# Four-direction convolution scan on one core: the DRAM layout of the inputs and of layer 0's results, and what is transferred in one DMA

## The chip, the cores and the metric

One core of a Trainium2 chip runs the whole program in one launch. The metric is device time in microseconds (us). Three runs of the kernel before took 4221.05, 4223.90 and 4226.26 us, so the median is 4223.9 us.

## What is computed

The input `x` has 32 images of 48 channels, 64 rows and 128 columns, in float32. Two layers follow each other. Each adds to `x` a chain of four scans over its group-normalised input (16 groups of three channels, over the whole image):

```python
def step(w, b):
    def f(carry, inp):
        nxt = inp + _conv1d(carry, w, b)     # 5 taps, 48 channels to 48
        return (nxt, nxt)
    return f
...
_, d_rest = jax.lax.scan(step(down_w, down_b), d0, xs[1:])     # over rows, downwards
_, u_rest = jax.lax.scan(step(down_w, down_b), u0, seq)        # over rows, upwards
_, r_rest = jax.lax.scan(step(right_w, right_b), r0, ws[1:])   # over columns, to the right
_, l_rest = jax.lax.scan(step(left_w, left_b), l0, R[Ww - 2::-1])
...
x = x + _L0_conv_ref(_gn(x), ...)
x = x + _L1_conv_ref(_gn(x), ...)
```

A scan is serial: row h needs row h-1 of the same scan. A row scan convolves along the width, a column scan along the height.

## The kernel before

The images are taken in four groups of eight. A row phase does the scan down and up of one group (126 steps of nine 128x128 products on TensorE, each record a half of a float32 product, so 18 records a step, and three adds on VectorE at L865). A column phase does the scans to the right and left of a pair of groups (254 steps). `PHASES` gives the order of the twelve phases: rows 0-0, rows 0-1, columns 0-0, rows 0-2, rows 1-0, rows 0-3, columns 0-1, rows 1-1, rows 1-2, rows 1-3, columns 1-0, columns 1-1, where the first number is the layer and the second the group or pair. The text below counts them from 0. The tiles of TensorE's results bear the names: `step_02d` is layer 0, group 2, downwards, phase 3; `step_11d` is phase 7.

SBUF holds three slots of rows. In a row phase a partition is a pair of (column modulo 8, channel), and 8 x 48 = 384 pairs fill three tiles of 128, `o` = 0, 1, 2. In a column phase a partition is a pair of (row modulo 8, channel). The change from one to the other goes through DRAM, in runs of 32 numbers (128 bytes), which are 4 columns of 8 images. Because 48 channels do not divide 128, a tile consists of three or four `PIECES` (48, 32 or 16 partitions), ten in the three tiles, and most transfers are made piece by piece.

The DRAM tensors in question are `xin` (the permuted input of each group, layer 0's source), `mid` (layer 0's result, layer 1's source), and `upa` and `upb` (the results of the row phases of layers 0 and 1). They are touched by:

- `move_rows` (L657): loads or stores blocks of eight rows for a row phase, one DMA for each piece, so ten DMAs for eight rows and 80 for a group's 64 rows. Each has four quarters of the width in it. A store for the seam between a row and a column phase gives the quarter `q` and takes a quarter alone.
- `scale_rows` (L688): ScalarE normalises 16 loaded rows in place, 24 instructions.
- `load_residual` (L776) and `keep_result` (L790): in a column phase they bring a unit of the source and take a unit of the result to `mid`. A unit is one quarter, one group of the pair and one tile of 128 partitions, with 8192 bytes a partition. They issue one DMA for each piece, three or four in a unit. `load_residual` issues on the queue of SyncE (SP) in layer 0 and on that of ScalarE (ACT) in layer 1, all the others on SP.
- `x_put` and `put_out`: write the permuted input to `xin`.

The order of the work is written by hand. `at(t, ...)` places work at a step number, the agenda is sorted by it, and `in_order` chains the instructions of each engine in that order. A step number thus only sets the place in an engine's queue. SP runs ahead of TensorE where nothing holds it. `plan_rows` places the loads in four lots of 16 rows at `t0 + ahead[i]` and their scaling at `t0 + scaled[i]`. A DMA on SP or ACT waits for one of eight completion semaphores, which the two queues use in turn, so that it also waits for the landing of the DMA that had its semaphore last.

`first_group` (L1145 on) is written out by hand for the first group: it loads eight rows directly in a form with 48 partitions (`top`, in two sets), moves them to their places by products with shifted identities (`place_kernel`, L1210, and `rows_by_product`, L1243), and does the statistics, the permutation and the first rows in between.

Of the kernel before, what the change touches and what calls it, by code (L numbers as in the profile page):

```python
# [29 lines left out]
F32 = mybir.dt.float32  # L30
# [3 lines left out]
C = 48  # L34
# [8 lines left out]
E8 = 8  # L43
# [76 lines left out]
def kernel(  # L120
# [62 lines left out]
    mask_in = wt["left"].rearrange("p i n -> p (i n)")[:, 5 * FULL : 5 * FULL + NG * C]  # L183
# [4 lines left out]
    def kept(name):  # L188

        return [  # L190
            dram.tile([C, CHANNEL + PAD], F32, tag=f"{name}{g}", name=f"{name}{g}")[:, 0:CHANNEL]
            for g in range(NGRP)
        ]

    source = [
        [
            dram.tile([E8 * NQ, C, UNIT], F32, tag=f"xin{g}", name=f"xin{g}")
            for g in range(NGRP)
        ],
        kept("mid"),  # L200
    ]
    ups = [kept("upa"), kept("upb")]
    taps = [
# [23 lines left out]
    def x_by_row(t, e, h0, h1):  # L227

        t = t.rearrange("(i q) c (a e n) -> e a c i q n", i=E8, a=NH, e=E8)[e, h0 // E8]
        return t[:, h0 % E8 : h0 % E8 + h1 - h0].rearrange("c i q n -> c (i q) n")  # L230

    def x_by_col(t, e, j):


        return t[e * NQ + j]

    def x_put(t, r):


        t = t.rearrange("(i q) c (a n) -> i (c a) q n", i=E8, a=NH)[r % E8]  # L240
        return t.rearrange("(p r) q n -> r p q n", r=PR // E8)[r // E8]

    def by_col(t, e, j):
# [108 lines left out]
    def scaling(key, layer, g, averages, masks, slack=0):  # L352
# [41 lines left out]
        if not slack:  # L394
            far = ps[:, 1 + NG : 2 + NG]
            nc.vector.tensor_tensor(far, mean_p, ps[:, 0:1], ALU.subtract)
            nc.vector.tensor_tensor(dev, mean_p, ps[:, 0:1], ALU.subtract)
            nc.vector.tensor_tensor(far, far, dev, ALU.mult)
            nc.vector.tensor_tensor(dev, far, var_p, ALU.add)
            yield  # L400
            expand(var, dev[:, 0])
            yield
            nc.vector.tensor_scalar(var, var, GN_EPS, None, ALU.add)
            r0 = small("std")
            nc.scalar.activation(r0, var, AF.Sqrt)
            expand(mean, mean_p[:, 0])
            yield
            yield
            nc.vector.reciprocal(r0, r0)
            nc.vector.tensor_tensor(var, var, r0, ALU.mult)  # L410
            nc.vector.tensor_tensor(var, var, r0, ALU.mult)
            nc.vector.tensor_scalar(var, var, -0.5, 1.5, ALU.mult, ALU.add)
            nc.vector.tensor_tensor(scale, var, r0, ALU.mult)
            nc.vector.tensor_tensor(offset, mean, scale, ALU.mult)
            nc.vector.tensor_scalar(offset, offset, -1.0, None, ALU.mult)
            return
# [237 lines left out]
    def row(k, h):  # L654
        return row_views(k)[h // HALF][:, :, h % HALF]

    def move_rows(k, h0, h1, to_dram, q=None):  # L657

        _, layer, g = PHASES[k]
        view = row_views(k)[h0 // HALF]  # L660
        t = (ups if to_dram else source)[layer][g]
        for h in range(h0, h1, E8):
            end = min(h1, h + E8)
            for o in range(NG):
                for e, c0, c1, p0 in pieces(o):
                    here = view[p0 : p0 + c1 - c0, o, h % HALF : h % HALF + end - h]
                    if to_dram or layer:
                        there = by_row(t, e, h, end, q)[c0:c1]
                    else:
                        there = x_by_row(t, e, h, end)[c0:c1]  # L670
                    if q is None:
                        here = here.rearrange("p h (q n) -> p (h q) n", q=NQ)
                    else:
                        here = here[:, :, q * RUN : (q + 1) * RUN]
                    if to_dram:
                        dma(there, here)
                    else:
                        dma(here, there)
# [97 lines left out]
    def load_residual(k, j, i, nat):  # L776
        _, layer, pair = PHASES[k]
        o, half = UNITS[i]
        t = source[layer][2 * pair + half]
        for e, c0, c1, p0 in pieces(o):  # L780
            here = nat[p0 : p0 + c1 - c0]
            there = (by_col if layer else x_by_col)(t, e, j)[c0:c1]
            dma(here, there, nc.scalar if layer else None)

    def add_residual(k, j, i, nat, eng=nc.gpsimd):
        o, half = UNITS[i]
# [3 lines left out]
    def keep_result(k, j, i):  # L790
        _, layer, pair = PHASES[k]
        o, half = UNITS[i]
        for e, c0, c1, p0 in pieces(o):
            dma(
                by_col(source[1][2 * pair + half], e, j)[c0:c1],
                quarter(k, j)[p0 : p0 + c1 - c0, half, o],
            )

    def by_image(t):

# [344 lines left out]
    def first_group():  # L1145
# [3 lines left out]

        shift = wt["left"].rearrange("p i n -> p (i n)")  # L1150
        start = 7 * C // 3
        whole = shift[:, 0 : 2 * FULL + start - C // 3 + ODD]
        part = shift[:, whole.shape[-1] : whole.shape[-1] + FULL + ODD]
        SETS = ((0, C), (ODD, ODD + C))

        def selects(piece, s=0):
            e, c0, c1, o, p0 = piece
            t, at = (part, 0) if c0 and p0 else (whole, start - p0 + c0)
            p, q = SETS[s]
            return t[p:q, at + p : at + p + FULL]  # L1160

        rows = PR // 2
        four = E8 // 2
# [2 lines left out]
        stats = InputStats("x0", GB)  # L1166
        n = W * GB

        kernel = slot[slots(0)[0]][0:C, 0 : TAPS * C + 6]
        zeros = slot[slots(0)[0]][0:C, 512 : 512 + NG * FULL + 6]  # L1170

        def load_kernel():
            nc.vector.memset(zeros, 0.0)
            for j in range(TAPS):
                d, si = divmod(TAPS - 1 - j, 2)
                to = kernel[:, j * C : (j + 1) * C]
                dma(to, w[SIDES[si], 0, DOWN, d, SIDES[0]], nc.scalar if j % 2 else nc.sync)
            aside(kernel[:, TAPS * C :], bias[0:C].rearrange("c l k -> c (l k)"))

        def make_ident():  # L1180
            nc.vector.memset(shift[:, 0 : whole.shape[-1] + FULL + ODD], 0.0)
            for t, base in ((whole, start), (part, 2 * C - C // 3)):
                nc.gpsimd.affine_select(
                    t,
                    t,
                    pattern=[[1, t.shape[-1]]],
                    compare_op=ALU.not_equal,
                    fill=1.0,
                    base=-base,
                    channel_multiplier=-1,  # L1190
                )
            nc.gpsimd.memset(part[:, 0 : 2 * C], 0.0)
            nc.gpsimd.memset(part[:, 2 * C - C // 3 + ODD : 2 * C + ODD], 0.0)

        def place_kernel():
            for i in range(NG):
# [181 lines left out]
```

## Time and profile before

| what | us |
|---|---|
| median of three runs | 4223.9 |
| the profiled execution's own time | 4228.38 |
| its span | 4226.6 |
| TensorE busy | 4086.4 (97%) |
| first scan step on TensorE | 62.3 |
| last record of a step on TensorE | 4143.8 |
| phase 1 starts (tile `step_01d`) | 334.7 |
| phase 3 starts (`step_02d`) | 1096.5 |
| phase 4 starts (`step_10d`) | 1367.0 |
| phase 5 starts (`step_03d`) | 1619.3 |
| phase 7 starts (`step_11d`) | 2381.1 |
| phase 8 starts (`step_12d`) | 2643.7 |
| phase 9 starts (`step_13d`) | 2892.7 |
| phase 10 starts (`step_10r`) | 3141.8 |

The starts are the first records of these tiles on TensorE. Phase 8 and phase 9 have no wait in them and took 249.0 and 249.1 us for 126 steps, hence 1.976 us a step. The timeline of SP shows each group of DMA instructions with its start, the time from its first to its last end, its tensors and a count. The time of such a group divided by its count is the time that the queue gives to one DMA.

### The profile page before, as it was taken

The numbers are of one execution on the slowest core, as the hardware profiler recorded it, in microseconds if no ns is written. First come the engines' busy times: TensorE is split into PE (matmuls) and PEld (weight loads), VectorE is DVE, ScalarE is ACT, GpSimd is POOL, SyncE is SP. The second block draws the span as 40 slices with busy tenths as digits, with TensorE's granted clock in tenths as the row PEclk, the third lists the DMA queues.
The fourth block names the chain that finished last, engine by engine and source line by source line (L and its number), as shares of the span: only waits on it lengthen the run. The fifth ranks groups of instructions, "written<-read, shape, count | busy, mean of one in ns | idle before, by whom it ended". The sixth has DMA issues, their size and how long they took to land. (4 is left out here: it accounts for less than half of the span.)

```text
span 4226.6 us, 90155 instructions
## 1 busy us (share of the span) xinstructions
PE 4086.4 (97%) x36724; PEld 4055.0 (96%) x36724; DVE 2135.8 (51%) x6501; ACT 1287.5 (30%) x2525; POOL 791.2 (19%) x737
## 2 busy tenths in 40 slices
PE   8999999999999999999999999999999999999992
PEld 6999999999999999989999999999999999999992
DVE  5454444456644454444457654444444444444443
ACT  6844000536874633000016854503000012110122
POOL 3520010334322100010023310000000034410352
PEclk9999999999999999999999999999999999999996
DMA  9987669659979997259419979759188059899999
GB/s 293 236 174 115 110 126 209 216 148 250 208 187 172 199 151 126 41 102 202 84 48 265 203 144 156 114 80 161 32 147 182 1 99 246 236 260 156 177 202 182
DMA packets 2118431, 680.55 MB, mean 161 GB/s; under 512 B 2006416, under 2 KB 2056832, under 8 KB 2079616
## 3 DMA queue, kind: packets, MB, share of 16 engines
q1 hardware_dynamic: 2015504, 582.07, 69.0%
q10 hardware_dynamic: 99952, 87.20, 9.7%
q0 software_dynamic: 2560, 5.51, 0.5%
q8 instruction: 289, 4.73, 0.5%
q14 instruction: 126, 1.03, 0.1%
HBM read 397.77 MB, written 295.14 MB: 164 GB/s over the span
## 5 line engine op out<-in xcount | busy, mean ns | idle before, releaser
L688 ACT ACTIVATE arena<-arena,offset,scale 128x256 f32<-128x256 f32 (+2 forms) x840 | 582.3, 788 | 310.4 <-DMA arena<-mid 176.8
L788 POOL TENSOR_TENSOR arena<-arena 128x2048 f32<-128x2048 f32 x80 | 362.9, 4548 | 1442.6 <-PE step_10l L856 461.4
L637 POOL COPY arena<-arena 128x256 f32<-128x256 f32 x332 | 196.7, 660 | 443.1 <-DMA arena<-in_x 394.2
L575 ACT ACTIVATE early<-arena 128x256 f32<-128x256 f32 x192 | 129.5, 674 | 453.6 <-DMA arena<-xin 315.2
L856 PE MATMUL step_01r<-arena,early 128*128 128x128 f32 x2286 | 254.2, 275 | 10.0 <-DMA arena<-arena 5.4
L856 PEld LDWEIGHTS step_01r<-arena,early 128*128 128x128 f32 x2286 | 253.3, 187 | 10.9 <-DVE arena L865 6.0
L856 PE MATMUL step_00r<-arena,early 128*128 128x128 f32 x2286 | 253.5, 275 | 8.7 <-DMA arena<-arena 4.4
L856 PEld LDWEIGHTS step_00r<-arena,early 128*128 128x128 f32 x2286 | 252.8, 186 | 9.4 <-issue 4.8
L856 PE MATMUL step_11r<-arena,early 128*128 128x128 f32 x2286 | 251.5, 274 | 5.5 <-DVE arena L865 5.5
L856 PEld LDWEIGHTS step_11r<-arena,early 128*128 128x128 f32 x2286 | 251.0, 185 | 5.9 <-DVE arena L865 5.8
L856 PE MATMUL step_00l<-arena,wleft 128*128 128x128 f32 x2286 | 249.3, 272 | 0.0
L856 PE MATMUL step_01l<-arena,wleft 128*128 128x128 f32 x2286 | 248.7, 272 | 0.1
L856 PEld LDWEIGHTS step_00l<-arena,wleft 128*128 128x128 f32 x2286 | 248.7, 184 | 0.0
L856 PEld LDWEIGHTS step_01l<-arena,wleft 128*128 128x128 f32 x2286 | 248.4, 184 | 0.3 <-DVE arena L865 0.3
L856 PE MATMUL step_10l<-arena,wleft 128*128 128x128 f32 x2286 | 248.5, 272 | 0.0
L856 PE MATMUL step_10r<-arena,early 128*128 128x128 f32 x2286 | 248.5, 272 | 0.0
L856 PE MATMUL step_11l<-arena,wleft 128*128 128x128 f32 x2286 | 248.5, 272 | 0.0
L856 PEld LDWEIGHTS step_10l<-arena,wleft 128*128 128x128 f32 x2286 | 248.4, 184 | 0.0
L856 PEld LDWEIGHTS step_10r<-arena,early 128*128 128x128 f32 x2286 | 248.4, 184 | 0.0
L856 PEld LDWEIGHTS step_11l<-arena,wleft 128*128 128x128 f32 x2286 | 248.4, 184 | 0.0
L813 ACT COPY arena<-arena 128x256 f32<-128x256 f32 x172 | 99.5, 655 | 409.0 <-POOL arena L788 154.1
L260 ACT COPY early<-arena 128x1 f32<-128x1 f32 x2 | 0.4, 192 | 655.0 <-DVE arena L865 655.0
(200 smaller groups left out, 7090.7 us busy)
## 6 DMA issues: line engine op xcount, KB each, us to landing
xin<-arena SPq DMA_DIRECT2D x91, 512.0 KB, 4.2
arena<-in_x SPq DMA_DIRECT2D x18, 2048.0 KB, 11.0
arena<-xin SPq DMA_DIRECT2D x96, 384.0 KB, 8.7
mid<-arena SPq DMA_DIRECT2D x96, 384.0 KB, 8.1
arena<-mid SPq DMA_DIRECT2D x192, 192.0 KB, 4.3
upb<-arena SPq DMA_DIRECT2D x192, 192.0 KB, 3.9
arena<-upb SPq DMA_DIRECT2D x96, 384.0 KB, 12.4
arena<-xin SPq DMA_DIRECT2D x180, 192.0 KB, 4.3
```

The costliest lines, as they stand in the source:

```text
L260: fn(*args)
L575: nc.scalar.activation(junk[:, 0:n], view[:, b], AF.Identity, accum_out=self.sum[:, i, j : j + 1])
L637: copy(dst[:, r, q], src[:, r0 + r, q])
L688: nc.scalar.activation(args[0], args[0], AF.Identity, bias=args[2], scale=args[1])
L788: eng.tensor_tensor(unit, unit, nat, ALU.add)
L813: copy(by_w(perm)[:, a], src[:, a])
L856: nc.tensor.matmul(part(whole(ps[o])[0:m], -s), weights[:, i, at : at + m], part(src(i), s), start=seen[o] == 1, stop=seen[o] == left[o],)
```

## The change

- `xin` of groups 1 to 3 and `mid` of all groups are laid out as (quarter, (row modulo 8, channel), position), `whole`, instead of ((row modulo 8, quarter), channel, position) and (channel, all the rest). Group 0 keeps its layout (`first_x`). A unit is then one block with one partition after the other: `by_unit` gives it in one DMA, or in two for `o` = 2.
- `load_residual` and `keep_result` use `by_unit`; for group 0's `xin` the old pieces stay.
- `move_rows` loads a piece with four DMAs, one for each quarter, except for group 0. Stores are as before.
- `plan_rows` no longer issues 16 rows in one lot: it places six lots of one `o` and eight rows, 1.3 steps apart, from two steps earlier.
- The products of `first_group` contract over 128 partitions instead of 48, with zeros in the rest; for this the weights' place, the identities and two ranges of 32 partitions of `top` are cleared first.
- In `scaling` without slack, the products for the mean are issued before the square root and not after it.

```diff
+    def whole(name, g):
+        return dram.tile([NQ, E8 * C, UNIT], F32, tag=f"{name}{g}", name=f"{name}{g}")
+
+    first_x = dram.tile([E8 * NQ, C, UNIT], F32, tag="xin0", name="xin0")
     source = [
-        [
-            dram.tile([E8 * NQ, C, UNIT], F32, tag=f"xin{g}", name=f"xin{g}")
-            for g in range(NGRP)
-        ],
-        kept("mid"),
+        [first_x] + [whole("xin", g) for g in range(1, NGRP)],
+        [whole("mid", g) for g in range(NGRP)],
     ]
...
-    def x_by_col(t, e, j):
-        return t[e * NQ + j]
+    def by_quarter(t, e, h0, h1, q):
+        t = t[q].rearrange("(i c) (a e n) -> e a c i n", i=E8, a=NH, e=E8)[e, h0 // E8]
+        return t[:, h0 % E8 : h0 % E8 + h1 - h0]
+
+    def by_unit(t, o, j):
+        at = [(o * FULL, 0, FULL)]
+        if o == NG - 1:
+            at = [(6 * C, 0, 2 * C), (5 * C + C // 3, 2 * C, FULL)]
+        return [(t[j, r : r + p1 - p0], p0, p1) for r, p0, p1 in at]
...
             expand(var, dev[:, 0])
+            expand(mean, mean_p[:, 0])
             yield
             nc.vector.tensor_scalar(var, var, GN_EPS, None, ALU.add)
             r0 = small("std")
             nc.scalar.activation(r0, var, AF.Sqrt)
-            expand(mean, mean_p[:, 0])
...
-    def move_rows(k, h0, h1, to_dram, q=None):
+    def move_rows(k, h0, h1, to_dram, q=None, groups=range(NG)):
...
-            for o in range(NG):
+            for o in groups:
...
-                    if to_dram or layer:
+                    if to_dram:
                         there = by_row(t, e, h, end, q)[c0:c1]
+                    elif t is first_x:
+                        there = x_by_row(t, e, h, end)[c0:c1]
                     else:
-                        there = x_by_row(t, e, h, end)[c0:c1]
+                        for n in range(NQ):
+                            dma(
+                                here[:, :, n * RUN : (n + 1) * RUN],
+                                by_quarter(t, e, h, end, n)[c0:c1],
+                            )
+                        continue
...
-        for e, c0, c1, p0 in pieces(o):
-            here = nat[p0 : p0 + c1 - c0]
-            there = (by_col if layer else x_by_col)(t, e, j)[c0:c1]
-            dma(here, there, nc.scalar if layer else None)
+        queue = nc.scalar if layer else None
+        if t is first_x:
+            for e, c0, c1, p0 in pieces(o):
+                dma(nat[p0 : p0 + c1 - c0], t[e * NQ + j][c0:c1], queue)
+        else:
+            for there, p0, p1 in by_unit(t, o, j):
+                dma(nat[p0:p1], there, queue)
...
-        for e, c0, c1, p0 in pieces(o):
-            dma(
-                by_col(source[1][2 * pair + half], e, j)[c0:c1],
-                quarter(k, j)[p0 : p0 + c1 - c0, half, o],
-            )
+        for there, p0, p1 in by_unit(source[1][2 * pair + half], o, j):
+            dma(there, quarter(k, j)[p0:p1, half, o])
...
             for i in range(4):
-                at(t0 + ahead[i], move_rows, k, i * LOAD, (i + 1) * LOAD, False)
+                for n in range(2 * NG):
+                    h, o = i * LOAD + n // NG * E8, n % NG
+                    t = t0 + ahead[i] - 2 + 1.3 * n
+                    at(t, move_rows, k, h, h + E8, False, None, (o,))
...
-        kernel = slot[slots(0)[0]][0:C, 0 : TAPS * C + 6]
-        zeros = slot[slots(0)[0]][0:C, 512 : 512 + NG * FULL + 6]
+        kernel = slot[slots(0)[0]][:, 0 : TAPS * C + 6]
+        zeros = slot[slots(0)[0]][:, 512 : 512 + NG * FULL + 6]
 
         def load_kernel():
+            nc.vector.memset(kernel, 0.0)
             nc.vector.memset(zeros, 0.0)
+            for p0 in (C // 3 * 2, 2 * C):
+                eng = nc.vector if p0 == 2 * C else nc.gpsimd
+                eng.memset(top[p0 : p0 + 2 * C // 3], 0.0)
...
-            src = top[SETS[s][0] : SETS[s][1]]
-            src = src.rearrange("p b (r k e) -> p e r k b", k=NK, e=E8)
+            src = top.rearrange("p b (r k e) -> p e r k b", k=NK, e=E8)
```

Counted in the two programs, SP issues 1680 DMAs more for the loads of the seven row phases 1, 3, 4, 5, 7, 8 and 9 (320 instead of 80 in each) and 168 fewer for units; ACT issues 96 fewer. The bytes, and the 128-byte runs of the row loads, are the same in number.

More of the change, by code (lines that the diff above doesn't have):

```diff
@@ L182 @@
     mask_r = const([FULL, NG, FULL], "mask_r")
-    mask_in = wt["left"].rearrange("p i n -> p (i n)")[:, 5 * FULL : 5 * FULL + NG * C]
+    mask_in = wt["left"].rearrange("p i n -> p (i n)")[:, 7 * FULL : 7 * FULL + NG * C]
     mask_in = mask_in.rearrange("p (o n) -> p o n", o=NG)
@@ L230, in x_by_row @@
         return t[:, h0 % E8 : h0 % E8 + h1 - h0].rearrange("c i q n -> c (i q) n")
-    def x_by_col(t, e, j):
-        return t[e * NQ + j]
+    def by_quarter(t, e, h0, h1, q):
[6 more added lines that the diff above has]
+        return [(t[j, r : r + p1 - p0], p0, p1) for r, p0, p1 in at]
     def x_put(t, r):
-        t = t.rearrange("(i q) c (a n) -> i (c a) q n", i=E8, a=NH)[r % E8]
+        if t is first_x:
+            t = t.rearrange("(i q) c (a n) -> i (c a) q n", i=E8, a=NH)[r % E8]
+        else:
+            t = t.rearrange("q (i c) (a n) -> i (c a) q n", i=E8, a=NH)[r % E8]
         return t.rearrange("(p r) q n -> r p q n", r=PR // E8)[r // E8]
@@ L779, in load_residual @@
         t = source[layer][2 * pair + half]
-        for e, c0, c1, p0 in pieces(o):
-            here = nat[p0 : p0 + c1 - c0]
-            there = (by_col if layer else x_by_col)(t, e, j)[c0:c1]
-            dma(here, there, nc.scalar if layer else None)
+        queue = nc.scalar if layer else None
+        if t is first_x:
+            for e, c0, c1, p0 in pieces(o):
+                dma(nat[p0 : p0 + c1 - c0], t[e * NQ + j][c0:c1], queue)
+        else:
+            for there, p0, p1 in by_unit(t, o, j):
+                dma(nat[p0:p1], there, queue)
     def add_residual(k, j, i, nat, eng=nc.gpsimd):
@@ L1151, in first_group @@
         start = 7 * C // 3
-        whole = shift[:, 0 : 2 * FULL + start - C // 3 + ODD]
-        part = shift[:, whole.shape[-1] : whole.shape[-1] + FULL + ODD]
+        span = 2 * FULL + start - C // 3 - ODD
         SETS = ((0, C), (ODD, ODD + C))
@@ L1157, in selects @@
             e, c0, c1, o, p0 = piece
-            t, at = (part, 0) if c0 and p0 else (whole, start - p0 + c0)
-            p, q = SETS[s]
-            return t[p:q, at + p : at + p + FULL]
+            at = s * (span + FULL)
+            at += span if c0 and p0 else start - p0 + c0
+            return shift[:, at : at + FULL]
         rows = PR // 2
@@ L1174, in load_kernel @@
             for j in range(TAPS):
                 d, si = divmod(TAPS - 1 - j, 2)
-                to = kernel[:, j * C : (j + 1) * C]
+                to = kernel[0:C, j * C : (j + 1) * C]
                 dma(to, w[SIDES[si], 0, DOWN, d, SIDES[0]], nc.scalar if j % 2 else nc.sync)
-            aside(kernel[:, TAPS * C :], bias[0:C].rearrange("c l k -> c (l k)"))
+            aside(kernel[0:C, TAPS * C :], bias[0:C].rearrange("c l k -> c (l k)"))
         def make_ident():
-            nc.vector.memset(shift[:, 0 : whole.shape[-1] + FULL + ODD], 0.0)
@@ L1182, in make_ident @@
[L1182 to L1193, printed above, removed]
+            nc.vector.memset(shift[:, 0 : 2 * (span + FULL)], 0.0)
@@ new lines, in make_ident @@
+            for s, (p0, p1) in enumerate(SETS):
+                at = s * (span + FULL)
+                whole, part = shift[:, at : at + span], shift[:, at + span : at + span + FULL]
+                for t, base in ((whole, start), (part, 2 * C - C // 3)):
+                    nc.gpsimd.affine_select(
+                        t,
+                        t,
+                        pattern=[[1, t.shape[-1]]],
+                        compare_op=ALU.not_equal,
+                        fill=1.0,
+                        base=p0 - base,
+                        channel_multiplier=-1,
+                    )
+                other = slice(ODD, FULL) if p0 == 0 else slice(0, ODD)
+                nc.gpsimd.memset(shift[other, at : at + span + FULL], 0.0)
+                nc.gpsimd.memset(part[:, 0 : 2 * C], 0.0)
```

## The prediction

> **What bounds the kernel now.** I read the page first, then TensorE's waits, then the timelines of SP, ACT and TensorE at the longest wait of a row phase.
>
> ```profile
> span 4226.6 us, 90155 instructions
> ...
> PE 4086.4 (97%) x36724; PEld 4055.0 (96%) x36724; DVE 2135.8 (51%) x6501; ACT 1287.5 (30%) x2525; POOL 791.2 (19%) x737
> ...
> q1 hardware_dynamic: 2015504, 582.07, 69.0%
> ```
>
> TensorE runs the serial scan and is the bound. A change can help only in the 62.3 us before the first step, the 83 us after the last, and the few waits between; it hurts wherever it makes a step wait. SP's queue (q1) fills 69% of the DMA engines, mostly with 128-byte runs. The waits between:
>
> ```profile
> PE step_00d L856 <- DVE arena L865: 11.6, 7, 5.6
> PE step_02d L856 <- issue: 8.2, 3, 6.5
> PE step_11r L856 <- DVE arena L865: 5.5, 1, 5.5
> ...
> PE step_11d L856 <- DVE arena L865: 3.6, 1, 3.6
> ```
>
> `step_02d` and `step_11d` (phases 3 and 7) are row phases behind column phases. What makes phase 3 wait is seen on SP, ACT and PE:
>
> ```profile
> 1119.23 31.20 SPq L249 DMA_DIRECT2D arena<-xin  x23
> ```
> ```profile
> 1150.97 16.45 ACT L688 ACTIVATE arena<-arena,offset,scale 128x256 f32<-128x256 f32 x22 [2.61 <-PE step_02d L856]
> ```
> ```profile
> 1166.42 0.77 PE L856 MATMUL step_02d<-arena,early 128*128 128x128 f32 x2 [6.46 <-issue]
> ```
>
> (Columns: start, time from first to last end, instructions, idle time before and what ended it.) The first 20 of those 23 DMAs, up to 1147.2, load rows 32 to 47. ACT can finish scaling them only after the last has landed, and TensorE resumes at 1166.4. So from a lot's last issue to the resumed scan there are 19.2 us. The lot after it repeats this (1184.6 to 1203.2, 18.6 us). Row phases thus hang on when SP has issued their last lots, and two of seven already lose time to it. The price of the new loads' shape stands in the stores of one quarter, which have the same form (8 runs of 128 bytes on 48, 32 or 16 partitions), beside whole row loads:
>
> ```profile
> 567.51 4.96 SPq L249 DMA_DIRECT2D upa<-arena  x10
> ```
> ```profile
> 647.16 18.49 SPq L249 DMA_DIRECT2D upa<-arena  x33
> ```
> ```profile
> 2676.37 40.70 SPq L249 DMA_DIRECT2D arena<-mid  x40
> ```
>
> A whole row DMA takes 1.02 us of the queue and moves four times what a quarter DMA does in 0.50 (4.96/10) to 0.56 us (18.49/33). With whole loads the DMA engines' busy share is 1.14, with quarter stores (636.8 to 665.7) 0.62: these wait for the issuing, not for data.
>
> **What the Trainium skill says.** "DMA: Bandwidth & Descriptors", section "Issuing engines are not separate DMA queues", says that the sequencer's time to initiate a DMA "is usually small relative to the DMA itself". For a whole row load that holds (4.3 us to landing against 1.02 us), for a quarter it doesn't: 1.8 us to landing (median from 636.7 to 666) against 0.56 us leaves three in flight: here the trace disagrees. "TensorE: Matmul & The Clock Gate", section "Part 1: The HAM clock gate (the "warmup" mystery)", says that the clock is halved until some 3.4 us of sustained activity. The trace agrees, with one addition: 60 us of nearly unbroken products on 48 partitions didn't warm it. The last 14 of them (512 columns) took 13.10 us, 1.83 ns a column; the first 72 step records 10.94 us; 70 later ones 7.94 us with 128 columns each, 0.89 ns a column.
>
> **The change, part by part.** My sum is made against the profiled span of 4226.6 us.
>
> *Row loads per quarter.* I take 0.53 us a DMA, the middle of 0.50 and 0.56. The bounds are 0.46 (consecutive 8192-byte DMAs at 666 us, 0.46 us apart) and 0.72 (40 quarter stores from 636.8 to 665.7, waits for unit transfers included). Sixteen rows are 80 DMAs, 42.4 us; before, 20 to 28 us. TensorE uses sixteen rows in 16 x 1.976 = 31.6 us, so in the downward half SP is slower than the scan. Where SP had been ahead, that eats the lead; the rest is waiting, priced at a phase's last lots: rows 32 to 47 are due 63.2 us, rows 48 to 63 94.8 us after its start.
>
> Phase 1. Loads start at 252.7 (the last input pieces must be in DRAM) and 30 stores of phase 0 stand among them as before, 31.8 us. End: 252.7 + 320 x 0.53 + 31.8 = 454.1; scan resumes at 473.3; due 334.7 + 94.8 = 429.5. Wait 43.8 us.
> Phase 3. From 1027.8: 169.6 for rows and 30 unit DMAs between them at 0.46, 13.8: 1211.2, resumed at 1230.4, due 1191.3. Wait 39.1, of which 9.0 existed (6.46 + 0.73 + 0.77 + 1.02). Adds 30.1.
> Phase 4. Before, SP took 72.6 us from phase 3's last row load to phase 4's first (units, input pieces, weights), in part waiting for ACT, which moves too. Kept: 1283.8. Then 160 loads (84.8), 5 us of input pieces, 40 stores (41): 1414.6. Rows 32 to 47 are issued by 1457.0 and usable at 1476.2; due 1367.0 + 30.1 + 63.2 = 1460.3: 15.9. The last lot: 1499.4, usable at 1518.6, due 1507.8: 10.8. Together 26.7.
> Phase 5. After 82 us of other work (as before), 160 loads, 40 stores: 1707; lots end at 1749.6 and 1792.0, usable at 1768.8 and 1811.2. Start 1619.3 + 56.8 = 1676.1: waits 29.5 and 10.8, together 40.3.
> Phase 7. From 2310.4, counted without earlier delays: 169.6 + 23 units at 0.46 = 2490.6, usable at 2509.8, due 2475.9: 33.9, of which 4.6 existed. Adds 29.3.
> Phases 8 and 9. Before, SP idled from 2717 to 2782; this lead is used up just so: waits of 4 and 3 us.
> Sum 43.8 + 30.1 + 26.7 + 40.3 + 29.3 + 7 = 177 us.
>
> A long wait also cools the clock: at 98.1 us, after 5.65 us, 72 records took 10.35 instead of 7.94 us, 2.4 us. Only a phase's last wait counts; three more than now, 7 us. Behind SP's longer queue stand the row stores and input pieces, counted above; behind ACT's wait for rows its statistics, whose users come a phase later.
>
> *Spreading.* Six lots, 1.3 steps apart, change the order on SP, not its sum; SP is behind anyway, so two steps' earlier place gives nothing. I take zero; the seven phases bound it at 4 us a phase either way.
>
> *Units whole.* SP saves 168 DMAs, which lie in the phases 2 and 6 (credited above where they stand among row loads). A unit DMA of 1 MB lands later than its pieces, and the eighth DMA after it waits for that: 0 to 15 us in each of phases 3 and 7; I take 0. ACT saves 96 in phases 10 and 11. At the end ACT issues residual loads between copies, but the DMA engines' share is 1.15 from 3960 to 4140 and 1.29 after, so data bound the last 83 us: gain 0 to 10, I take 3. `step_11r`'s 5.5 us may go with it; included.
>
> *First group.* If 128 partitions warm the clock, the last 14 products take some 7 instead of 13.1 us and the first steps save 3.0 (10.94 - 7.94). But the loads of `top`, with all input behind them on SP, must wait for clearing 32 x 4096 numbers. Before, 608 columns took VectorE 0.56 us, hence 3.8 us: 2 us later than now. Scaling by VectorE until 59.4 us then ends near 61.5, and the waits for group 0's rows at 74 to 112 us stay. Bounds: -4 (warm), +7 (still cold: clearing delays the placing products, which fill TensorE to 43.4 us). I take 0. The mean's six products (1.45 us) now come before the root instead of after it, where VectorE waited 1.20 us for them: what is saved behind is spent ahead, 0, within 1.4 us either way.
>
> Total 4226.6 + 177 + 7 - 3 = 4408; the profiled execution's own time was 4228.4, 4.5 above the median, so 4410 - 4.5, rounded: **4405 us**.
>
> **The rivals.** *A, the loads stay hidden* (ends on the other side: not slower). Phase 1 has no wait if 320p + 31.8 fits into 429.5 - 19.2 - 252.7, p up to 0.39 us. DMAs 0.35 us apart occur right after an idle queue (608.84 to 609.19), which speaks for it; long rows at 0.50 speak against. Then clock and units remain: 4224 - 4 - 10 = 4210. *B, issuing is cheap but not enough*: at 0.46, the same ledger gives 21 + 8 + 4 + 18 + 7 = 58, less 7: about 4275. The 8192-byte row speaks for it, the extra dimension of these DMAs against. *C, units and rows block each other* through the eight semaphores: at 0.60 and 15 us more in phases 3 and 7 it gives 66 + 67 + 50 + 62 + 67 and, as the lead no longer suffices, 46 in phases 8 and 9, 358: 4580. The 0.72 speaks for it; there, unit transfers ran beside.
>
> **How the numbers follow.** Forecast (0.49 to 0.57, 4320 to 4520) 0.66, A 0.06, B 0.14, C 0.14. The range, 4280 to 4520, takes in B's upper half. Differences up to 0.2% (8 us) can't be told from none. Faster: 0.05 of A's 0.06. Within: the other 0.01 and 0.01 at B's lower end. Slower: the rest, 0.93.
>
> **What would show it.** Right: SP's row loads in groups of 80 in some 42 us; waits of 10 to 40 us of `step_01d`, `step_02d`, `step_10d`, `step_03d`, `step_11d`; DMA share near 0.6 while SP issues rows; phases 10 and 11 unchanged; the first 14 late products near 7 us. Wrong: row loads under 0.40 us each, or scaling that no longer waits for whole lots.

## The result

The changed kernel takes 4472.56 us (median of four runs, 4462.77 to 4476.32), the kernel before, run beside it, 4222.48: a ratio of 1.059, with a 95% interval of 1.0569 to 1.0611. It is slower by 250 us, where 181 were forecast. The profiled execution took 4471.97 us with a span of 4469.8, so 243.2 us more span than before.

The page of the changed kernel:

```profile
span 4469.8 us, 92001 instructions
...
PE 4119.4 (92%) x36724; PEld 4076.3 (91%) x36724; DVE 2145.1 (48%) x6503; ACT 1288.6 (29%) x2525; POOL 791.9 (18%) x742
...
q1 hardware_dynamic: 2039696, 582.17, 62.0%
...
arena<-mid SPq DMA_DIRECT2D x768, 48.0 KB, 2.0
```

TensorE's share falls from 97% to 92%, and SP's queue, with 24,192 more packets but nearly the same bytes, fills the DMA engines less (62% of the span, 69% before). So the slower kernel doesn't move more; more time passes without work. TensorE's waits say where (time in all, times, longest):

```profile
PE step_02d L876 <- DVE arena L885: 48.9, 5, 32.0
PE step_10d L876 <- DVE arena L885: 39.5, 5, 31.1
PE step_11d L876 <- DVE arena L885: 38.9, 5, 22.5
PE step_03d L876 <- DVE arena L885: 28.3, 4, 19.5
PE step_02d L876 <- issue: 26.0, 1, 26.0
PE step_11d L876 <- issue: 23.2, 1, 23.2
PE step_01d L876 <- DMA arena<-xin: 18.8, 1, 18.8
PE step_01d L876 <- DVE arena L885: 18.0, 5, 8.3
```

These are the five row phases that the forecast named. The timeline of SP in phase 7 shows the loads behind two of the waits, and the first ones of phase 8:

```profile
2685.75 25.43 SPq L262 DMA_DIRECT2D arena<-mid  x40
...
2711.72 22.12 SPq L262 DMA_DIRECT2D arena<-mid  x40
...
2776.69 86.88 SPq L262 DMA_DIRECT2D arena<-mid  x160
```

The last line is a stretch of row loads alone: 86.88/160 = 0.543 us each, and the windows view gives a DMA busy share of 0.47 for it, even less than the 0.6 that I had named as a sign. Where unit transfers stand between them (the two lines above), one takes 0.64 and 0.55 us, and 40 of them are only eight rows. What then follows is the same as before. ScalarE scales after the last load, and TensorE goes on when it is through; ACT's and TensorE's timelines at a wait of phase 3:

```profile
1256.02 16.29 ACT L708 ACTIVATE arena<-arena,offset,scale 128x256 f32<-128x256 f32 x22 [5.24 <-DMA arena<-xin]
```
```profile
1271.33 0.77 PE L876 MATMUL step_02d<-arena,early 128*128 128x128 f32 x2 [25.95 <-issue]
```

The table sets the phases side by side: differences between the first records of each phase's tile on TensorE, in us.

| stretch | before | after | difference | forecast |
|---|---|---|---|---|
| to the first step | 62.3 | 67.8 | +5.5 | 0 |
| phase 0 | 272.4 | 273.3 | +0.9 | 0 |
| phase 1 | 253.5 | 301.6 | +48.1 | +43.8 |
| phase 2 | 508.3 | 503.2 | -5.1 | 0 |
| phase 3 | 270.4 | 340.3 | +69.9 | +30.1 |
| phase 4 | 252.4 | 306.5 | +54.1 | +26.7 |
| phase 5 | 253.4 | 288.8 | +35.4 | +40.3 |
| phase 6 | 508.3 | 506.3 | -2.0 | 0 |
| phase 7 | 262.6 | 326.6 | +64.0 | +29.3 |
| phases 8, 9 | 498.1 | 505.2 | +7.1 | +7 |
| phases 10, 11 | 1001.9 | 994.2 | -7.7 | 0 |
| after the last step | 82.8 | 56.1 | -26.7 | -3 |

The forecast's 7 us for a cooled clock lie inside the phases. The seven row phases lost 278.6 us against 184 (clock included), and the rest gained 35.1 against 3.

The end is best seen in the windows view, from 190 us before the last step to it, and from there to the end (length, busy time of PE, PEld, DVE, ACT and POOL, granted clock, DMA share, GB/s). The kernel before:

```profile
3953.80:4143.80 190.00, 189.99 (x1750) 189.79 (x1748) 93.36 (x292) 43.41 (x75) 109.81 (x69) 1.00 1.13 193
4143.80:4226.60 82.80, 0.00 (x0) 0.00 (x0) 25.10 (x19) 18.89 (x33) 20.75 (x22) 0.52 1.30 178
```

The changed kernel:

```profile
4223.70:4413.70 190.00, 190.00 (x1750) 189.84 (x1748) 93.36 (x292) 49.20 (x85) 113.89 (x72) 1.00 1.12 216
4413.70:4469.80 56.10, 0.04 (x1) 0.00 (x0) 25.13 (x19) 13.31 (x23) 12.74 (x18) 0.53 1.27 171
```

The share is the same (1.13 and 1.12), but in that share 216 GB/s move instead of 193. In 190 us these are 4.4 MB more, which no longer remain after the last step.

### The profile page after: what moved, and what is told of

The parts are those of the page before. It is cut to its first block, busy times and chain, and to the rows that moved or that the text cites. A ratio compares the mean times of both kernels' runs of the same rounds, so it can differ in the third digit from the quotient of the medians.

```text
span 4469.8 us, 92001 instructions
## 1 busy us (share of the span) xinstructions
PE 4119.4 (92%) x36724; PEld 4076.3 (91%) x36724; DVE 2145.1 (48%) x6503; ACT 1288.6 (29%) x2525; POOL 791.9 (18%) x742
## 3 DMA queue, kind: packets, MB, share of 16 engines
q14 instruction: 138, 1.13, 0.1%
## 5 line engine op out<-in xcount | busy, mean ns | idle before, releaser
L876 PEld LDWEIGHTS step_01r<-arena,early 128*128 128x128 f32 x2286 | 252.5, 186 | 10.2 <-DVE arena L885 5.3
L876 PE MATMUL step_02d<-arena,early 128*128 128x128 f32 x1134 | 135.0, 283 | 74.9 <-DVE arena L885 48.9
## 6 DMA issues: line engine op xcount, KB each, us to landing
arena<-mid ACTq DMA_DIRECT2D x29, 1024.0 KB, 10.3
```

The source lines that it names most:

```text
L876: nc.tensor.matmul(part(whole(ps[o])[0:m], -s), weights[:, i, at : at + m], part(src(i), s), start=seen[o] == 1, stop=seen[o] == left[o],)
```

## The experiments

The theory: the row loads per quarter are bound by SP's issuing, at 0.54 us each, and SP is then slower than the scan. The rivals: the layout makes the loads slower; units and rows block each other; the order of the lots or the new head costs the time. All ratios are to the kernel before on the same chip.

**Row loads per quarter alone, from the kernel before**

```diff
-                    there = ...                      # one DMA for a piece
+                    for n in range(NQ):
+                        dma(here[:, :, n * RUN : (n + 1) * RUN], by_row(...)[..., n])
```

> Only the row loads are split by quarter (as in the changed kernel), with the old layouts, the old units in pieces, the old lots and the old first group. Theory (SP's issuing of four times as many DMAs is the cost): the waits of step_01d, step_02d, step_10d, step_03d and step_11d come as in the changed kernel, and the gain at the end does not: 4222 plus some 270 = 4490 us (4450 to 4540), tail of 83 us as before. Rival (the new layout makes the small reads slow, or whole units block the rows): with the old layout little is lost, under 4300 us.

Measured: 4539.93 us, ratio 1.0753 (1.0728 to 1.0778). In the old layout the loads cost even more than the whole change (+320 us against +250). Phases 1, 3, 4, 5 and 7 took 306.4, 346.9, 307.3, 289.5 and 345.8 us, like those of the changed kernel or longer. The layout isn't the cause; the four DMAs in place of one are enough.

**The lots of 16 rows at their old places, in the changed kernel**

```diff
-                for n in range(2 * NG): ... at(t0 + ahead[i] - 2 + 1.3 * n, move_rows, k, h, h + E8, False, None, (o,))
+                at(t0 + ahead[i], move_rows, k, i * LOAD, (i + 1) * LOAD, False)
```

> The changed kernel with the loads of 16 rows placed in one lot again, no spreading. Theory (the queue's sum counts, not its order): 4472 within 15 us. Rival (loads spread among units make the mixed stretches slow): phases 3 and 7 lose their extra 35 us each, 4400 us.

Measured: 4465.88 us, ratio 1.0579 (1.0561 to 1.0598), 6.7 us (0.15%) less than the changed kernel, which can't be told from none. If the spreading costs or brings something, it is too small to be seen here.

**One DMA for the four quarters, in the changed kernel**

```diff
-                        for n in range(NQ): dma(here[:, :, n * RUN : (n + 1) * RUN], by_quarter(t, e, h, end, n)[c0:c1])
+                        there = t.rearrange("q (i c) (a e n) -> e a c (q i) n", ...)[e, h // E8][c0:c1]
+                        dma(here, there)
```

> The changed kernel, but each piece of eight rows is loaded by one DMA again, from the same tensor with the same 128-byte runs in the same number. To be one DMA it takes the runs in the order (quarter, row) where the place in SBUF has (row, quarter), so rows and quarters are interchanged in the loaded data and the result is another one; all else is the changed kernel. Theory (the number of DMAs is all of the loss): the row phases are as in the kernel before; what else the change does stays: end shorter by 27 us, phases 2, 6 and 11 by 15, start later by 6: 4222 - 36 = 4186 us (4170 to 4215). Rival (layout or whole units slow the rows): phases 3 and 7 still wait 20 us or more each, over 4222 us.

Measured: 4182.57 us, ratio 0.9909 (0.9891 to 0.9927). Phases 1, 3, 4, 5 and 7 are back at 254.9, 265.2, 251.2, 253.5 and 256.0 us, with the same bytes from the same places; rows and quarters only come to lie interchanged in SBUF, which makes the result another one and changes no transfer in size. Of the long waits of phase 3 one short one is left:

```profile
PE step_02d L875 <- issue: 7.1, 2, 6.4
```

This is the most direct proof: the number of DMAs costs some 290 us, and the rest of the change gains some 37 (4219.74 for the kernel before on the same chip).

**The old head, in the changed kernel**

```diff
-    first_group with 128 partitions and cleared ranges
+    first_group of the kernel before (48 partitions)
```

> The changed kernel with the first group's products on 48 partitions as before. Theory (clearing delays the input, the warm clock gives little): the first step starts at 62 instead of 68 us and all shifts by 5 to 6 us: 4466 us. Rival (the warm clock pays): 3 us or more slower than the changed kernel, 4476 us.

Measured: 4463.46 us, ratio 1.0579 (1.0556 to 1.0601). The first step comes at 62.0 us instead of 67.8. The new head costs some 6 us; the whole times lie too close together to show it.

**Odd quarters on ScalarE's queue, in the changed kernel**

```diff
-                            dma(here[...], by_quarter(...))
+                            dma(here[...], by_quarter(...), nc.scalar if n % 2 else nc.sync)
```

> The changed kernel, with the odd quarters of each row load issued on ACT's queue, the even ones on SP's as before. Theory (each queue's own issuing, 0.54 us a DMA, is the pace, and the DMA engines have room at a share of 0.47): 80 DMAs in some 22 to 25 us instead of 43, most of the waits of phases 1, 3, 4, 5 and 7 go; ACT pays 0.5 us of its time for each of 160 DMAs a phase, so some waits for scaling stay: 4230 to 4320 us. Rival (one thing shared by both queues, the making of descriptors or the eight semaphores, sets the pace): the pace of both together stays at 0.54 us, 4450 us or more.

Measured: 4365.60 us, ratio 1.0345 (1.0329 to 1.0360), below the rival's time and above mine. Two fifths of the loss are gone. The timelines of SP and of ACT in phase 8:

```profile
2795.30 46.43 SPq L262 DMA_DIRECT2D arena<-mid  x80
```
```profile
2792.36 40.27 ACTq L262 DMA_DIRECT2D arena<-mid  x67
2832.81 35.75 ACT L709 ACTIVATE arena<-arena,offset,scale 128x256 f32<-128x256 f32 x48 [40.93 <-DMA arena<-mid]
```

Each queue takes its 0.58 and 0.60 us for one DMA, while the other does the same: the pace belongs to the queue, and two together issue nearly twice as much. What I had not priced is that the scaling stands behind ACT's own DMAs (40 us here). Ahead of the statistics at 1099.9, for instance, it was taken up by its own DMAs for 35.9 us. Phases 2, 3 and 7 took 538.7, 317.2 and 307.4 us: ACT became what the scan waits for.

**Residual loads in the old pieces, from the new layout**

```diff
-            for there, p0, p1 in by_unit(t, o, j):
-                dma(nat[p0:p1], there, queue)
+            for e, c0, c1, p0 in pieces(o):
+                dma(nat[p0 : p0 + c1 - c0], t[j, e * C + c0 : e * C + c1], queue)
```

> The changed kernel, but load_residual takes a unit in the old three or four pieces from the new tensors, in both layers. Theory for the end (8192-byte packets on ACT's queue took 602 ns before and 425 ns in the changed kernel because the new tensor is read in address order): the end stays near 56 us and the whole at 4472 within 15. Rival (one large DMA instead of three or four is what counts): the end goes back to 80 us or more, 4497 us.

Measured: 4535.78 us, ratio 1.0749 (1.0733 to 1.0764). My theory for the end, that the new addresses make the residual loads cheaper, is wrong; the rival, that whole transfers do, is right. The end is 82.4 us as before the change, and the windows view shows the old 196 GB/s in the old share:

```profile
4263.70:4453.70 190.00, 190.00 (x1750) 189.85 (x1748) 93.40 (x292) 43.40 (x75) 113.04 (x71) 1.00 1.15 196
4453.70:4536.10 82.40, 0.04 (x1) 0.00 (x0) 24.18 (x19) 18.88 (x33) 13.69 (x20) 0.52 1.24 171
```

Phases 7 and 11 got 17 and 11 us longer too. So it isn't that a unit is one large DMA which makes phases 3 and 7 so slow: the same bytes in pieces are no better.

**The kernel before, with a second copy of layer 0's result for the units**

```diff
+    copies = [... [NQ, E8 * C, UNIT] for each group]
+    def copy_mid(g, j):      # one DMA, DRAM to DRAM
+        dma(copies[g][j].rearrange("(i c) n -> c i n", i=E8), source[1][g].rearrange("c (i q n) -> q c i n", ...)[j])
...
-    row loads and residual loads from one tensor
+    row loads as before; layer 1's residual loads by whole unit from copies
```

> The kernel before, with a second copy of mid in the changed kernel's layout, made by 16 DMAs from DRAM to DRAM where SP's queue is idle (phases 8, 9 and 10), and read by load_residual in layer 1 in whole units. All else as before. Theory (whole units from that layout shorten the end, and phase 11's wait goes): end 56 us instead of 83, phase 11 shorter by 8: 4220 - 34 = 4186 us (4175 to 4205). Rival (the copies delay the row stores and loads behind them on SP, or the end's gain needs a shorter queue elsewhere): 4215 us or more.

Measured: 4183.13 us, ratio 0.9912 (0.9896 to 0.9927). It beats both kernels, the one before by 0.9%. The 16 copies of 3 MB,

```profile
copy<-mid SPq DMA_DIRECT2D x16, 3072.0 KB, 26.1
```

lie where SP's queue was idle (after 2717 and later); phases 8 to 10 keep their 249.0, 249.1 and 496.7 us, the end takes 54.4 us, and in the 190 us before it 216 GB/s move at a share of 1.11. The change's gain at the end can be had without its cost.

**Two DMAs for the four quarters**

```diff
-                        dma(here, there)
+                        for n in (0, 16): dma(here[:, n : n + 16], there[:, n : n + 16])
```

> As the version with one DMA for each piece of eight rows (rows and quarters interchanged in the loaded data, so another result), but each of these DMAs cut in two of 16 runs. Theory (issuing costs nothing until its 0.53 us pass the DMA engines' own time, which for half a piece is 1.02/2 = 0.51 us): 160 DMAs a phase in some 85 us, about as one, 4183 plus 0 to 20 us. Rival (each DMA adds its cost): a third of the distance to the changed kernel, 4183 + 96 = 4279 us.

Measured: 4199.52 us, ratio 0.9951 (0.9937 to 0.9965), 17 us above one DMA, where four cost 290. So it isn't one price per DMA: the first doubling costs 17 us, the second 273. A threshold fits: the scan uses sixteen rows in 31.6 us. With two DMAs for a piece SP issues them in 40 x 0.60 = 24 us (47.77 us for 80), with four in 80 x 0.543 = 43.4.

**The units of layer 0 on GpSimd's queue, in the changed kernel**

```diff
-        queue = nc.scalar if layer else None
+        queue = nc.scalar if layer else nc.gpsimd
...
-            dma(there, quarter(k, j)[p0:p1, half, o])
+            dma(there, quarter(k, j)[p0:p1, half, o], nc.gpsimd)
```

> The changed kernel, with the unit transfers of layer 0 (load_residual and keep_result in phases 2 and 6) issued on GpSimd's queue instead of SP's. Their bytes, their moment and the number of row loads stay; they no longer stand between the row loads of phases 3 and 7 on SP, and no longer share the eight completion semaphores with them. Theory: a row load behind a unit waits for the unit's landing, because it reuses its semaphore. Then the 320 row loads of phases 3 and 7 go at 0.54 us, 173 us instead of 235, and the two phases lose some 55 to 62 us each: 4345 to 4365, with the waits of phases 3 and 7 near those of phase 1. Rival: the DMA engines are shared with the units' data, whichever queue issues them: the row loads stay at 0.65 us or more beside the units, phases 3 and 7 stay at 325 to 345, 4450 to 4480. In between, 4370 to 4440, both have a part, or GpSimd's own work (permuting, adding, copying) is delayed by the issuing.

Measured: 4466.15 us, ratio 1.0566 (1.0548 to 1.0583). In time this is the rival's case, in the phases neither: phases 3 and 7 took 310.6 and 311.8 us, but 2 and 6 took 523.9 and 520.7. The 320 row loads of phase 3 ran from 1053.6 to 1297.5, 243.9 us and not 173. GpSimd issued its last unit at 1183.7. After that SP's timeline shows

```profile
1192.96 104.54 SPq L262 DMA_DIRECT2D arena<-xin  x199
```

0.525 us each. The 121 before took 1.15, since they must also wait until the column results have left the places that they are loaded to: 18.4 us of SP's waits there end with `bn_r`, VectorE's statistics of these results. The run mixes the two effects, so the next three leave the places out.

**Additional units between the row loads of phase 8, large and small**

```diff
+    def extra_unit(i):
+        dma(stage[:, i], source[1][0][i, 0:FULL])       # small: stage[:, i, 0:RUN], ...[i, 0:FULL, 0:RUN]
...
                     at(t, move_rows, k, h, h + E8, False, None, (o,))
+                    if k == 8 and n % 2:
+                        for m in range(2): at(t + 0.01, extra_unit, m + 2 * (n // 2 % 2))
```

> The changed kernel, with 24 additional loads of a whole unit (128 partitions, 1 MB, out of group 0's result in mid into the four residual buffers, which nothing uses then) in twelve pairs between the row loads of phase 8, on SP. Nothing waits for them and no row load needs their places, so that only the queue, the completion semaphores and the DMA engines can let them slow the row loads. Without them 160 row loads take 86.9 us, and the issuing of twelve units adds 5.5. Theory (a small load that follows a unit waits until the unit has landed, because it reuses its semaphore or stands behind its data): each of the six pairs in a stretch costs 3 to 5 us more, so 110 to 122 us for such a stretch, 0.65 us or more for a row load, and phase 8 grows by 20 to 60 us. Rival (the slow stretches of phases 3 and 7 come from row loads whose places the column results still occupy, not from the transfers beside them): 90 to 95 us a stretch, phase 8 at most 10 us longer.

> The same 24 additional loads in phase 8, but of 128 bytes a partition (16 KB) instead of 8192. This is the control for their number: as many issues and as many semaphores, hardly any data. If size is what blocks, a stretch of 160 row loads with twelve of them takes 92 to 95 us, and phase 8 grows by at most 10. If it is their number or the change between two kinds of transfers, it takes as long as with whole units.

Measured: large 4529.97 us, ratio 1.0728 (1.0705 to 1.0752), phase 8 303.8 us; small 4484.27 us, ratio 1.0630 (1.0609 to 1.0652), phase 8 262.9. SP's timeline with large units, 160 row loads and 12 units a line:

```profile
2775.21 112.28 SPq L262 DMA_DIRECT2D arena<-mid  x172
...
2933.78 110.84 SPq L262 DMA_DIRECT2D arena<-mid  x172
```

and with small ones:

```profile
2776.92 94.06 SPq L262 DMA_DIRECT2D arena<-mid  x172
...
2910.95 94.29 SPq L262 DMA_DIRECT2D arena<-mid  x172
```

Against 86.88 us without, a large unit between row loads costs (112.28 - 86.88)/12 = 2.1 us of SP, a small one 0.6; the second stretch, 85.82 us without, gives 2.1 and 0.7. So the bytes make 1.5 of the 2.1 us and the mere number 0.6, and no places are involved. The landing shows it too: in the first stretch the slowest row load took 3.8 us from issue to landing without units, 3.6 with small ones and 9.3 with large ones.

**The same large units, issued by GpSimd**

```diff
     def extra_unit(i, k, h, o):
+        nc.gpsimd.tensor_copy(stage[:, i, 0:1], row_views(k)[h // HALF][:, o, h % HALF, N - 1 : N])
-        dma(stage[:, i], source[1][0][i, 0:FULL])
+        dma(stage[:, i], source[1][0][i, 0:FULL], nc.gpsimd)
```

> As in the run with 24 additional whole units in phase 8, but GpSimd issues them on its own queue, each after a copy of one number of the row block that stood before it, so that they start at the same points between the row loads. Size, number and moment are as there; queue and completion semaphores are no longer shared with the row loads. There a stretch of 160 row loads with twelve units took 112.3 and 110.8 us, with twelve small ones 94, without any 86.9. Theory 1 (a row load waits for a semaphore that a unit holds, or is behind a unit in its queue): the stretches take 86 to 91 us, phase 8 at most 5 us longer than the 250.4 of the changed kernel, 4465 to 4485 in all. Theory 2 (the DMA engines share their time between the unit's data and the row loads, whichever queue they come from, so that row loads land late and their own semaphores stay taken): 103 us or more, phase 8 at 280 to 305, 4500 to 4530. Between 92 and 102 us both have a part.

Measured: 4528.31 us, ratio 1.0719 (1.0701 to 1.0737). SP's timeline:

```profile
2773.91 109.19 SPq L262 DMA_DIRECT2D arena<-mid  x160
...
2931.51 108.55 SPq L262 DMA_DIRECT2D arena<-mid  x160
```

Theory 2, by its number: although units and rows share neither queue nor semaphores now, 160 row loads take 22 us more beside twelve units, and the slowest of the first stretch landed after 10.2 us. The semaphores that they shared aren't the cause. What they still share are the DMA engines and the DRAM behind them, which no run here separates. "DMA: Bandwidth & Descriptors" of the Trainium skill, section "Issuing engines are not separate DMA queues", says that all DMAs run on the same 16 engines and interleave there, whichever engine started them. Here the trace agrees. The whole time says less than the stretches: phase 7 took 347.9 us and phase 8 282.0, since GpSimd's copies wait for row loads and its own share of the statistics, `dev_r`, stood behind them (TensorE waited 16.0 us for it).

## Why the prediction was right, and where its sizes were off

**The mechanism was right.** The pace was taken as 0.53 us from stores of the same form and measured as 0.543. The 19.2 us from a lot's last issue to the resumed scan nearly held: the loads that ended at 1254.4 were followed by the scan at 1271.3 (16.9), those that ended at 1606.9 at 1623.7 (16.8). Phase 1's loads and the stores among them took 201.6 us (259.2 to 460.8) where the ledger had 201.4. Phases 1, 5, 8 and 9, where few other transfers stand among the row loads, came out as worked out: +48.1, +35.4 and +7.1 against 43.8, 40.3 and 7. Rival A (hidden loads) and B (0.46 us) are out by the pace; that spreading is worth about zero came out as taken.

**Mis-sized: "30 unit DMAs between them at 0.46, 13.8" and the unit blocking, "0 to 15 us in each of phases 3 and 7; I take 0".** The 320 loads and the 30 unit DMAs of phase 3 took 234.9 us (1069.6 to 1304.5) where the ledger had 183.4. At 0.543 us the loads alone are 173.8, so that the unit DMAs cost 61 us and not 13.8, far outside my bound of 15 more. Only 17 MB are in these 30 DMAs, since group 0's units still come in pieces and the third tile in two parts. With the prices measured since, 0.6 us for a DMA and 1.5 us for each MB, I estimate 30 x 0.6 + 17 x 1.5 = 44 us of the 61. Phase 7, with 23 DMAs and again 17 MB, took 231.0 us from 2502.8 to 2733.8 instead of 180.2: 57 us for the units, of which the same prices give 39. Some 18 us in each phase thus stay open.

So in phases 3 and 7 rival C came true in size (67 and 67 forecast by it, 69.9 and 64.0 measured), but by luck: it had a pace of 0.60 and 15 us of blocking, and for phases 1, 5 and 8 with 9 it gave 66, 62 and 46, where they lost 48.1, 35.4 and 7.1. Nor does the blocking need semaphores that units and rows share.

I had read the busy share of 0.62 as room for the units. It is a mean. After the units that SP issued from 1105.9 to 1107.7 the engines are full for 7 us, and the row load right behind them landed after 8.5 us, where those before them had taken about 2. The windows view (columns as above) has these 7 us and the 10 us after them:

```profile
1109.00:1116.00 7.00, 7.00 (x67) 7.00 (x67) 4.90 (x14) 6.72 (x18) 2.55 (x1) 1.00 1.02 265
1116.00:1126.00 10.00, 10.00 (x95) 10.00 (x94) 7.70 (x22) 7.20 (x16) 2.01 (x1) 1.00 0.49 76
```

**Mis-sized: phase 4, "5 us of input pieces".** The first 160 loads with their five transfers of input ran for 106.9 us, from 1375.4 to 1482.3, where the ledger had 89.8: most likely the same effect. The third lot's wait became 31.1 us instead of 15.9, the last one 6.8 instead of 10.8. Another 6.9 us come from VectorE, where the step's additions stood behind statistics of an input piece that had come late (its instruction at L536 waited 4.13 us for ACT, the next one took 3.60); that input pieces stand behind SP's longer queue I had named and taken as counted. The remaining 9 us or so are short waits and a cooler clock (286 records in 34.04 us after the long wait, 31.4 at the pace of a phase without waits).

**Wrong: "data bound the last 83 us: gain 0 to 10, I take 3".** The gain was 26.7 us. The share of 1.13 did show that the engines were busy throughout, but not that their work was as small as it could be: the pieces moved 193 to 196 GB/s in it, whole units 216. The piece run and the copies show that this comes from the whole transfers. "SBUF — State Buffer" of the Trainium skill, section "Door 1: The DMA port swizzle", says that a transfer's bandwidth depends on how many of SBUF's 16 ports its partitions reach, all with 128 partitions, half of them with the first 64. The direction agrees; no run here counts ports. Phases 2, 6 and 11 gained 5.1, 2.0 and 7.7 us; in phase 11 the 5.5 us wait of `step_11r` went, as allowed for.

**Off within its bounds: the head, "I take 0", bounds -4 and +7.** It cost 5.5 us. Clearing was the dearer case: the first products start at 8.34 us instead of 2.63. The clock did warm, but the 14 products didn't go faster by it, and here the prediction had misread a line: it took their 1.83 ns a column for a cold clock. Six small products shortly before them show the warm clock, on TensorE's timeline of the kernel before and of the changed one:

```profile
45.93 1.42 PE L374 MATMUL ps_x<-dev_x,maskp 128*128 128x8 f32 x6 [0.96 <-DVE dev_x L399]
```
```profile
53.66 0.81 PE L387 MATMUL ps_x<-dev_x,maskp 128*128 128x8 f32 x6 [0.96 <-DVE dev_x L412]
54.99 12.98 PE L1272 MATMUL rows<-arena,wleft 128*128 128x512 f32 x14
67.79 8.08 PE L876 MATMUL step_00d<-arena,early 128*128 128x128 f32 x72
```

The 14 products take 12.98 us as in the old form (13.10), not the 7 that I had named as a sign. While they run, the granted clock of the changed kernel is first half, then full (windows view):

```profile
55.30:58.70 3.40, 3.40 (x5) 0.95 (x4) 2.90 (x11) 1.64 (x6) 3.04 (x6) 0.50 1.09 385
58.70:67.80 9.10, 9.10 (x12) 2.07 (x11) 6.70 (x13) 7.17 (x15) 8.79 (x16) 1.00 1.08 378
```

In both stretches these records start 0.91 us apart, as they do in the kernel before. So their pace isn't the clock's; what sets it no run here shows. The clock itself follows the form of the products: the trace of the kernel before has its first record of a full clock at 68.1 us, that of the changed kernel at 31.4. In the other twelve runs it comes at 66.8 to 67.6 us with the old head (three runs) and at 12.2 to 17.6 with the new one (nine). (The windows view counts time without a record as full.) What the warm clock brings are the 72 step records after the 14 (8.08 us instead of 10.94), and later waits in phase 0 take that back.

In sum the row phases were 95 us too cheap and the rest 32 us too dear in the forecast, which brings +181 to +243 in the span. What stays open: the exact way in which a unit holds up the small loads (each also waits for one of its own eight semaphores, which late landings keep taken), why the five transfers of input in phase 4 cost some 20 us for 4 MB, twice as much for a megabyte as the added units of 1 MB do, and how much of the 18 us in phases 3 and 7 comes from stores, from transfers close together or from places still occupied.

## What to carry to other kernels

Count DMAs for each consumer's period, not bytes: as long as a queue issues a lot faster than the scan uses it, halving the size costs next to nothing, and where it issues more slowly than that, the DMAs are on the path. Price small transfers beside large ones by their mixed pace, and don't take a mean busy share below one as room. A busy share above one is no proof that the end can't get shorter: compare GB/s at equal share, and if one side wants whole blocks and the other whole rows, a second copy made in an idle stretch can serve both.

## What the runs showed of the hardware that I had not expected

- A row load of 8 x 128 bytes a partition (48 KB at most) takes 0.543 us of its queue; two queues side by side take 0.58 and 0.60 each, so together one in some 0.3 us.
- A 1 MB load between such loads costs their queue 2.1 us, and nearly as much (22.3/12 = 1.9 us) when it comes from another queue with semaphores of its own. A load of 16 KB in its place costs 0.6.
- The same 1 MB unit in whole transfers instead of pieces of 48, 32 or 16 partitions raises what is moved at an equal DMA share from 196 to 216 GB/s, a tenth.
- 60 us of products on 48 partitions left the clock cold; the same products on 128 partitions, with zeros in the added ones, did not: the first full clock on record comes at 66.8 to 68.1 us in the four runs with the old head and at 12.2 to 31.4 in the ten with the new one, and the 72 step records take 10.3 to 10.9 us there and 8.08 here.
- The 512-column products of the head start 0.91 us apart at half the clock and at the full clock alike. A long record is thus no proof of a cold clock.
